# Moving h by squares in runs of 1 KB, for block 0 too, with block 0's first products reordered

## The chip, the cores and the metric

The kernel runs on one core of a Trainium2 chip. The metric is the device time of one execution in microseconds (us); before the change it is 526.12 us, the median of 3 runs (525.29 to 526.21).

The engines have short names in the profile: PE is TensorE (PEld its weight loads), DVE is VectorE, ACT is ScalarE, POOL is GpSimd, SP is SyncE, whose queue (SPq) issues most of the transfers (DMAs). Each engine works through its own instructions in order; semaphores hold an instruction until what it needs is done.

## The reference

Two layers with residuals and a layer norm after each. The input is 8192 tokens of 256 features.

```python
def _L0_attn_ref(x, W_q, W_k, W_v, W_g, W_o, log_decay):
    ...
    S = jnp.einsum('bncd,bnkd->bnck', Qc, Kc) * mask        # chunks of 32 tokens
    O = jnp.einsum('bnck,bnkd->bncd', S, Vc).reshape(B, T, D)
    gate = jax.nn.sigmoid(x @ W_g.T)
    out = gate * O @ W_o.T + x
    return out

def _L0_ffn_ref(x, w_gate, w_up, w_down):      # 768 hidden, integer weights * 1/127
    ...
    h = jax.nn.silu(gate) * up
    return jnp.einsum('bsh,dh->bsd', h, wd)

x = L0_attn_x
x = _layernorm(x + _L0_attn_ref(x, ...), axis=-1)
x = _layernorm(x + _L0_ffn_ref(x, ...), axis=-1)
```

All of it is float32. What the kernel calls h is x after the first layer norm, the input of the second layer.

## The kernel before

The tokens are worked on in 16 blocks of 512 (`TB`). A tile has the 128 partitions of the memory in front; a block of token-major data is four groups (`NG`) of 128 tokens by 256 features.

For each block the attention part makes v, y (the queries times one product of W_q and W_k), the gate, the scores (`attn_scores`, tile ps), their values (`attn_values`, po, goT) and the projection back (`attn_residual`, pa, or `split_out`, p_o). Most of these 256 x 256 products use a scheme with seven products instead of eight on halves (`seven`): first p1, p6, p5, p7, and in a second half, `rest`, three more onto the same banks. It needs sums of the input's quarters beforehand, which POOL makes (`token_sums`: t1, t3, t2, t4 on lines 444 to 447). Product p6 reads t2, the third of them.

The second layer splits its input h and its weights into a high part (32-bit) and a low part (16-bit). `ffn_up` makes, for each of six chunks of 128 hidden features, a gate bank and an up bank (fg, fu), each from two high and two low products, one for each half of the features (`dc`); the sigmoid (s, ACT), two multiplications (s and u, DVE), the high part of u (u_hi, ACT) and the low part (u_lo, POOL) follow. `ffn_down` (fdn) projects back and adds h.

`ffn_up` needs h with features on the partitions (hT), while the layer norm leaves it with tokens there. Two ways are in the kernel:

- `transpose_h`, for blocks 0 and 15: PE transposes (tile pt, eight of 128 x 128), ACT copies the high part, DVE makes the low part.
- `move_h` and `split_h`, for blocks 1 to 14: ACT normalizes h group by group (`normalize`, line 410), DVE transposes squares of 32 x 32 in place (`nc.vector.transpose`, tile sq), SP issues 16 transfers of 32 KB that bring the squares to their partitions (hT), then ACT casts the high part (line 772) and POOL makes the low part (line 773). sq and hT have one buffer each.

In `move_h` before, each transfer has for each of its 32 partitions two runs of 512 bytes on both sides.

Blocks are interleaved: while block b goes through the second layer, block b+2 has its scores, values and projection, and block b+3 its v, y and gate. Ahead of the loop, the first blocks are started by hand, and block 0's h goes by `attn_out` (its layer norm on DVE, the root on ACT) and `transpose_h`. There the order on the engines is a planner's, except where a line says `in_turn` (or `order`, which is then `in_turn`): such instructions keep the program's order. `steady` does the same for most of DVE's instructions from block 1 on. The planner also places the work of POOL and SP, so that the built order can differ from the program's.

ACT's functions come in tables that are loaded when another function is called (ACT_TABLE_LOAD); a tiny activation on the tile `table` loads one ahead of its use. `scale_and_shift` makes the factors of a layer norm from a root by ACT; `iterated_scale_and_shift` makes them on POOL with a power and one step of iteration.

PSUM has 8 banks, all from one pool (`bank`).

Of the kernel before, what the change touches and what calls it, by code (L numbers as in the profile page):

```python
# [47 lines left out]
F32 = mybir.dt.float32  # L48
# [3 lines left out]
AF = mybir.ActivationFunctionType  # L52
ALU = mybir.AluOpType

P = 128
CHUNK = 32
PAIR = 2 * CHUNK
SQ = 32
# [13 lines left out]
def kernel(  # L72
# [36 lines left out]
    def bank(name):  # L109
        return psum.tile([P, TB], F32, tag="ps", name=name)  # L110
# [190 lines left out]
    def in_turn(ins):  # L301
        tc.keep_in_program_order(ins)
# [75 lines left out]
    def iterated_scale_and_shift(mv, kind, name):  # L378
        on_r, on_dst = kind

        def column(tag):
            return small.tile([P, NG], F32, tag=tag, bufs=2, name=f"{tag}_{name}")

        def times(out, a, b):
            nc.gpsimd.tensor_tensor(out, a, b, ALU.mult)

        def line(out, a, slope, at_0):
            nc.gpsimd.tensor_scalar(out, a, slope, at_0, ALU.mult, ALU.add)

        v, y, t, minus, shift = map(  # L390
            column, ("v", "y", "t", "minus_mean", "term")
        )
        in_turn(
            nc.vector.tensor_scalar(
                v, mv[:, :, 1], 1 / on_dst**2, EPS * (on_r / on_dst) ** 2, ALU.mult, ALU.add
            )
        )
        nc.gpsimd.tensor_tensor(y, v, half, ALU.pow)
        nc.gpsimd.tensor_scalar(minus, mv[:, :, 0], -1.0, None, ALU.mult)
        times(t, y, y)  # L400
        times(t, t, v)
        line(t, t, -0.5, 1.5)
        times(y, y, t)
        times(shift, y, minus)
        return y, shift
# [33 lines left out]
    def token_sums(t, name, order=free):  # L439

        out = sums.tile([P, 4, HB], F32, tag=f"{name[0]}_sums", name=f"{name}_sums")
        t1, t3, t2, t4 = (out[:, i, :] for i in range(4))
        b11, b12, b21, b22 = (t[:, k, n * HB : (n + 1) * HB] for k in range(2) for n in range(2))
        order(nc.gpsimd.tensor_tensor(t1, b12, b11, ALU.subtract))
        nc.gpsimd.tensor_tensor(t3, b22, b12, ALU.subtract)
        nc.gpsimd.tensor_tensor(t2, b22, t1, ALU.subtract)
        nc.gpsimd.tensor_tensor(t4, t2, b21, ALU.subtract)
        return b11, b21, b22, t4, t1, t2, t3
# [173 lines left out]
    def attn_scores(b, yT):  # L622
        xt = xTs.pop(b)
        halves = [slice(i * PAIR, (i + 1) * PAIR) for i in range(P // PAIR)]
        ps = bank(f"ps_{b}")[:, : NG * PAIR].rearrange("p (g c) -> p g c", c=PAIR)
        for g in range(NG):
            for fc in range(KD):
                for rows in halves:
                    tokens = slice(g * P + rows.start, g * P + rows.stop)
                    nc.tensor.matmul(  # L630
                        ps[rows, g, :],
                        lhsT=xt[:, fc, tokens],
                        rhs=yT[:, fc, tokens],
                        start=(fc == 0),
                        stop=(fc == KD - 1),
                    )
        sTs.append(sTs.pop(0))
        sT = sTs[-1]
        for rows in halves:
            in_steady_turn(  # L640
                nc.vector.tensor_tensor(sT[rows, :, rows], ps[rows], mask[rows], ALU.mult)
            )
        return sT.rearrange("p g c -> p (g c)")
# [59 lines left out]
    def attn_out(b, goT):  # L703
        r = attn_residual(b, goT)
        layer_norm(r, f"a{b}", on_r=HALF, on_dst=H_UP)
        return r
# [33 lines left out]
    def move_h(b, h):  # L740

        sq = moved.tile([P, D // SQ, NG, SQ], F32, tag="sq", name=f"sq_{b}")
        for g in range(NG):
            in_turn(
                nc.vector.transpose(
                    sq[:, :, g, :], h[:, g, :].rearrange("p (j f) -> p j f", f=SQ)
                )  # L750
            )
        hT = moved.tile([P, KD, NQ, NG * SQ], F32, tag="hT", name=f"hT_{b}")
        for q in range(NQ):
            for j in range(NQ):
                nc.sync.dma_start(
                    hT[j * SQ : (j + 1) * SQ, :, q, :],
                    sq[q * SQ : (q + 1) * SQ, j::NQ, :, :].rearrange(
                        "p k g t -> p k (g t)"
                    ),
                )  # L760
        return hT

    def split_h(b, hT):
        hi = work.tile([P, KD, TB], F32R, tag="hT_hi", name=f"hT_hi_{b}")
        lo = work.tile([P, KD, TB], F16, tag="hT_lo", name=f"hT_lo_{b}")
        for dc in range(KD):
            whole = hT[:, dc, :, :].rearrange("p q (g t) -> p g q t", g=NG)
            in_order = [
                part[:, dc, :].rearrange("p (g q t) -> p g q t", g=NG, q=NQ)
                for part in (hi, lo)  # L770
            ]
            tc.keep_in_program_order(nc.scalar.copy(in_order[0], whole))  # L772
            nc.gpsimd.tensor_tensor(  # L773
                in_order[1], whole, in_order[0].bitcast(F32), ALU.subtract
            )
        return hi, lo


    def ffn_up(b, hT, uT, chunks, cols=slice(0, TB), held=False, order=free):

        n = cols.stop - cols.start
        for hc in chunks:
            pg = bank(f"fg_{b}_{hc}_{cols.start}")[:, :n]
            pu = bank(f"fu_{b}_{hc}_{cols.start}")[:, :n]

            kinds = (0, 1) if hc % 2 == 0 else (1, 0)
            for kind in kinds:
                for pb, w in ((pg, fg), (pu, fu)):
                    for dc in range(KD):
                        nc.tensor.matmul(  # L790
                            pb,
                            lhsT=w[kind][:, dc, hc * P : (hc + 1) * P],
                            rhs=hT[kind][:, dc, cols],
                            start=(kind == kinds[0] and dc == 0),
                            stop=(kind == kinds[1] and dc == KD - 1),
                        )
            s = work.tile([P, n], F32, tag="s", name=f"s_{b}_{hc}")
            order(nc.scalar.activation(s, pg, AF.Sigmoid, scale=SCALE / H_UP))  # L798

            gated = nc.vector.scalar_tensor_tensor(  # L800
                s, pg, U_UP / H_UP**2, s, ALU.mult, ALU.mult
            )
            in_steady_turn(gated)
            if len(uT[0]) == hc:
                for kind, dtype, tiles in zip(("hi", "lo"), (F32R, F16), uT):
                    tiles.append(
                        acts.tile([P, TB], dtype, tag=f"u_{kind}", name=f"u_{kind}_{b}_{hc}")
                    )

            def multiply(hc=hc, pu=pu, s=s):  # L810
                u = work.tile([P, n], F32, tag="u", name=f"u_{b}_{hc}")
                in_steady_turn(nc.vector.tensor_tensor(u, pu, s, ALU.mult))  # L812
                hi, lo = uT[0][hc][:, cols], uT[1][hc][:, cols]
                nc.scalar.copy(hi, u)  # L814
                nc.gpsimd.tensor_tensor(lo, u, hi.bitcast(F32), ALU.subtract)  # L815

            if held:
                return multiply
            multiply()
# [103 lines left out]
    goT = attn_values(0, sT, v, sg)  # L923
    rest()
    fd = integers(ffn_dT, ffn_int[2], "fd")
    hs[0] = attn_out(0, goT)
    sT_1 = attn_scores(1, yT)
    xTs[3] = load_xT(3)
    x_sums = token_sums(xTs[2], "x_2")
    v, rest = split_v(2, x_sums)  # L930
    goT = attn_values(1, sT_1, v_1, sg_1)
    go_sums = token_sums(goT, "go_1")
    rest()
    yT, rest = split_y(2, x_sums)
    hTs[0] = transpose_h(0, hs[0])
    in_turn(nc.scalar.activation(table, eps, AF.Sigmoid))
    rest()
    hs[1], out_rest = split_out(1, go_sums)
    sg, g_rest = split_gate(2, x_sums)
    scales_h = iterated_scale_and_shift(out_rest(), of_h, "h_1")  # L940
    ahead = yT, v, sg

# [9 lines left out]
    for b in range(NB - 2):  # L952
# [1 line left out]
        m = b + 3  # L954
        more = m < NB
        xns[n] = load_xn(n)
        hT = hTs.pop(b)
        uT = [], []
        yT, v, sg = ahead
        steady = b > 0  # L960
        if b:
            normalize(hs[b + 1], *scales_h)
            moving = move_h(b + 1, hs[b + 1])
        ffn_up(b, hT, uT, range(0, 1))
        if b == 0:
            g_rest()
            x_sums = token_sums(xTs[m], f"x_{m}")
        ffn_up(b, hT, uT, range(1, 2))
        sT = attn_scores(n, yT)
        if m + 1 < NB:  # L970
            xTs[m + 1] = load_xT(m + 1)
        ffn_up(b, hT, uT, range(2, 3))
        if b == 0:

# [283 lines left out]
```

## Time and profile before

| what | value |
|---|---|
| median of 3 runs | 526.12 us (525.29 to 526.21) |
| the profiled execution, its time | 525.69 us |
| its span, first to last instruction | 524.1 us |
| mean granted TensorE clock | 0.997 of full |
| transfers hT<-sq | 224 (16 in each of 14 blocks), 32 KB each |
| x and xT loads | 512 KB each |

How to read the profile: a row of a timeline has the start in us, the length in us, the engine, the line of the kernel, the operation, out<-in with the names of the tiles, and a count where like instructions are merged; in brackets is the idle time before it and what ended that. The row of slices has one digit for each fortieth of the span, the busy share in tenths; PEclk is the granted clock in tenths. An answer for one tile or line gives the durations in ns, as least, median and most. The chain in order of time has start, length and what held the end up in that stretch. Ends of matmuls are modelled, and they overlap in the pipeline: the pitch of two products is less than the length of one.

### The profile page before, as it was taken

How to read it: one execution, taken by the hardware profiler on the slowest of the kernel's cores; microseconds unless marked ns; L12 is line 12 of the kernel's file. 1: busy time of each engine (PE TensorE's matmuls, PEld its weight loads, DVE VectorE, ACT ScalarE, POOL GpSimd, SP SyncE). 2: the span in 40 equal slices, each digit the busy share in tenths (PEclk: the TensorE clock that was granted, in tenths of full speed). 3: DMA queues.
4: the chain of work that ended last, by engine and by line, in shares of the span. 5: the costliest groups of instructions: out<-in, count | busy, mean ns of one | idle time of the engine just before them, and what ended most of it. 6: DMA issues, size and time to landing. Idle time of an engine off the chain costs nothing.

```text
span 524.1 us, 10570 instructions
## 1 busy us (share of the span) xinstructions
PE 517.6 (99%) x3648; PEld 422.9 (81%) x3648; DVE 390.0 (74%) x963; ACT 322.4 (62%) x644; POOL 342.5 (65%) x476
## 2 busy tenths in 40 slices
PE   9999999999999999999999999999999999999995
PEld 5798887887978788887888878889787888878684
DVE  3878797676776867868677776867868677787876
ACT  2755565465656756666575665756567566667745
POOL 7435785776847668485675857668486685836554
PEclk9999999999999999999999999999999999999998
DMA  7621121212313131131312313131121311102102
GB/s 259 215 88 43 51 60 28 65 41 61 103 31 91 52 111 41 40 89 50 105 43 45 119 25 97 46 114 43 35 89 51 110 43 39 44 20 62 62 26 78
DMA packets 43320, 36.90 MB, mean 70 GB/s; under 512 B 4864, under 2 KB 39168, under 8 KB 43264
## 3 DMA queue, kind: packets, MB, share of 16 engines
q1 hardware_dynamic: 42288, 35.41, 23.1%
q10 hardware_dynamic: 976, 0.79, 0.5%
q8 instruction: 30, 0.49, 0.4%
q14 instruction: 26, 0.21, 0.1%
HBM read 20.45 MB, written 8.39 MB: 55 GB/s over the span
## 4 chain that ended last, share of the span: by engine, by line
PE 96%; DVE 2%; ACT 1%; POOL 1%; issue 0%; DVEq 0%; ACTq 0%
PE fg L790 16%; PE fu L790 16%; PE fdn L677 14%; PE p_v L473 9%; PE p_y L455 9%; PE p_g L455 9%; PE p_o L473 8%; PE po L651 5%; PE ps L630 3%; PE fdn L856 2%; PE pa L677 1%; PE pi L185 1%; PE pg L570 1%; PE pv L610 1%; PE py L589 1%; DVE st_f L322 0%
## 5 line engine op out<-in xcount | busy, mean ns | idle before, releaser
L815 POOL TENSOR_TENSOR u_lo<-u,u_hi 128x512 f16<-128x512 f32 (+1 forms) x98 | 122.9, 1256 | 111.7 <-ACT u_hi L814 109.5
L814 ACT CAST u_hi<-u 128x512 fp32r<-128x512 f32 (+1 forms) x98 | 59.7, 609 | 65.5 <-DVE u L812 65.2
L800 DVE SCALAR_TENSOR_TENSOR s<-fg,s 128x512 f32<-128x512 f32 (+1 forms) x98 | 65.9, 673 | 34.3 <-ACT s L798 34.1
L798 ACT ACTIVATE s<-fg 128x512 f32<-128x512 f32 (+1 forms) x98 | 57.0, 582 | 41.6 <-PE fg L790 41.5
L812 DVE TENSOR_TENSOR u<-fu,s 128x512 f32<-128x512 f32 (+1 forms) x98 | 66.5, 679 | 11.1 <-POOL u_lo L815 1.0
L790 PE MATMUL fg<-hT_hi,fg_hi 128*128 128x512 f32 (+1 forms) x196 | 74.0, 458 | 0.0
L790 PE MATMUL fu<-hT_hi,fu_hi 128*128 128x512 f32 (+1 forms) x196 | 60.5, 390 | 0.0
L790 PE MATMUL fg<-hT_lo,fg_lo 128*128 128x512 f16 (+1 forms) x196 | 58.0, 377 | 0.0
L790 PE MATMUL fu<-hT_lo,fu_lo 128*128 128x512 f16 (+1 forms) x196 | 57.5, 375 | 0.0
L677 PE MATMUL fdn<-fd_hi,u_hi 128*128 128x256 f32 x312 | 46.9, 292 | 0.0
L790 PEld LDWEIGHTS fu<-hT_hi,fu_hi 128*128 128x128 f32 x196 | 36.5, 188 | 8.5
L790 PEld LDWEIGHTS fg<-hT_hi,fg_hi 128*128 128x128 f32 x196 | 34.6, 189 | 8.8
L410 ACT ACTIVATE h<-h,shift_h,scale_h 128x256 f32<-128x256 f32 x52 | 27.0, 589 | 23.6 <-POOL shift_h L373 23.6
L677 PEld LDWEIGHTS fdn<-fd_hi,u_hi 128*128 128x128 f32 x312 | 39.8, 189 | 0.3
L677 PE MATMUL fdn<-fd_lo,u_lo 128*128 128x256 f16 x312 | 38.6, 273 | 0.0
L790 PEld LDWEIGHTS <-fu_lo 128*128 128x128 f16 x196 | 19.2, 98 | 22.2
L838 DVE SCALAR_TENSOR_TENSOR r<-fdn,h 128x512 f32<-128x512 f32 x30 | 20.7, 689 | 21.3 <-PE fdn L677 19.1
L773 POOL TENSOR_TENSOR hT_lo<-hT,hT_hi 128x512 f16<-128x512 f32 x28 | 35.3, 1283 | 1.2 <-ACT hT_hi L772 1.2
L790 PEld LDWEIGHTS <-fg_lo 128*128 128x128 f16 x196 | 15.3, 98 | 20.6 <-issue 12.9
L677 PEld LDWEIGHTS <-u_lo 128*128 128x128 f16 x312 | 28.4, 98 | 4.2
L473 PE MATMUL p_v<-v_sums,x_sums 128*128 128x128 f32 x240 | 31.7, 275 | 0.0
L651 PE MATMUL po<-sT,v 128*128 128x128 f32 x256 | 31.2, 275 | 0.0
(206 smaller groups left out, 1184.0 us busy)
## 6 DMA issues: line engine op xcount, KB each, us to landing
x<-in_x_dram SPq DMA_DIRECT2D x16, 512.0 KB, 3.5
xT<-in_xT_dram SPq DMA_DIRECT2D x15, 512.0 KB, 4.3
hT<-sq SPq DMA_DIRECT2D x224, 32.0 KB, 1.9
out_dram<-r SPq DMA_DIRECT2D x13, 512.0 KB, 4.7
out_dram<-r SPq DMA_DIRECT2D x8, 128.0 KB, 1.7
fg_int<-in_ffn_gT_dram SPq DMA_DIRECT2D x3, 256.0 KB, 7.9
fu_int<-in_ffn_uT_dram SPq DMA_DIRECT2D x3, 256.0 KB, 7.1
fd_int<-in_ffn_dT_dram SPq DMA_DIRECT2D x3, 256.0 KB, 6.0
```

Source lines behind the costliest of these rows:

```text
L410: nc.scalar.activation(r[:, g, :], r[:, g, :], AF.Identity, bias=shift[:, g : g + 1], scale=scale[:, g : g + 1],)
L455: nc.tensor.matmul(pb, lhsT=a[i - 1], rhs=b[i - 1], start=first, stop=True, skip_group_check=True,)
L473: nc.tensor.matmul(pb[:, g * P : (g + 1) * P], lhsT=b[i - 1][:, g * P : (g + 1) * P], rhs=a[i - 1], start=first and g == 0, stop=True, ski ...
L651: nc.tensor.matmul(po[:, cols], lhsT=v[:, g, dc * P : (dc + 1) * P], rhs=sT[:, cols], start=True, stop=True,)
L677: nc.tensor.matmul(pb[:, j * D : (j + 1) * D], lhsT=part[:, g * P : (g + 1) * P], rhs=w, start=(i == 0), stop=(i == len(terms) - 1),)
L773: nc.gpsimd.tensor_tensor(in_order[1], whole, in_order[0].bitcast(F32), ALU.subtract)
L790: nc.tensor.matmul(pb, lhsT=w[kind][:, dc, hc * P : (hc + 1) * P], rhs=hT[kind][:, dc, cols], start=(kind == kinds[0] and dc == 0), stop=( ...
L798: order(nc.scalar.activation(s, pg, AF.Sigmoid, scale=SCALE / H_UP))
L800: gated = nc.vector.scalar_tensor_tensor(s, pg, U_UP / H_UP**2, s, ALU.mult, ALU.mult)
L812: in_steady_turn(nc.vector.tensor_tensor(u, pu, s, ALU.mult))
L814: nc.scalar.copy(hi, u)
L815: nc.gpsimd.tensor_tensor(lo, u, hi.bitcast(F32), ALU.subtract)
```

## The change

- `move_h`: sq and hT are laid out so that each transfer has one run of 1 KB for each of its 32 partitions on both sides: the quarter of the features (j, or q on the other side) now stands ahead of the half (k). DVE's transposes write in that order, `split_h` reads in it. The number of transfers, their bytes and the 16 issues stay.
- Block 0's h goes the same way. Its layer norm is made by `root`, `scale_and_shift` and `normalize`; `move_h(0, ...)` stands ahead of `attn_values(1, ...)`, and `split_h(0, ...)` takes the place of `transpose_h(0, ...)`. ACT's table for the root is loaded ahead of `attn_residual(0, ...)`, and that for the sigmoids after the normalizing.
- In block 0 the second half of the gate of block 2 (`g_rest`), the token sums of block 3 and the scores of block 2 stand ahead of the first up products.
- `ffn_up` has a new mode for block 0's first two chunks: all high products of both chunks first, then the low ones. Four banks are open meanwhile.
- Some instructions on POOL get `in_turn`: the power and the negated mean of the iterated layer norm, and the second of the token sums.

The diff, cut to its core:

```diff
-        nc.gpsimd.tensor_tensor(y, v, half, ALU.pow)
-        nc.gpsimd.tensor_scalar(minus, mv[:, :, 0], -1.0, None, ALU.mult)
+        in_turn(nc.gpsimd.tensor_tensor(y, v, half, ALU.pow))
+        in_turn(nc.gpsimd.tensor_scalar(minus, mv[:, :, 0], -1.0, None, ALU.mult))
...
-        nc.gpsimd.tensor_tensor(t3, b22, b12, ALU.subtract)
+        order(nc.gpsimd.tensor_tensor(t3, b22, b12, ALU.subtract))
...
-        sq = moved.tile([P, D // SQ, NG, SQ], F32, tag="sq", name=f"sq_{b}")
+        sq = moved.tile([P, NQ, KD, NG, SQ], F32, tag="sq", name=f"sq_{b}")
         for g in range(NG):
             in_turn(
                 nc.vector.transpose(
-                    sq[:, :, g, :], h[:, g, :].rearrange("p (j f) -> p j f", f=SQ)
+                    sq[:, :, :, g, :].rearrange("p j k t -> p k j t"),
+                    h[:, g, :].rearrange("p (k j f) -> p k j f", j=NQ, f=SQ),
                 )
             )
-        hT = moved.tile([P, KD, NQ, NG * SQ], F32, tag="hT", name=f"hT_{b}")
+        hT = moved.tile([P, NQ, KD, NG * SQ], F32, tag="hT", name=f"hT_{b}")
         for q in range(NQ):
             for j in range(NQ):
                 nc.sync.dma_start(
-                    hT[j * SQ : (j + 1) * SQ, :, q, :],
-                    sq[q * SQ : (q + 1) * SQ, j::NQ, :, :].rearrange(
-                        "p k g t -> p k (g t)"
-                    ),
+                    hT[j * SQ : (j + 1) * SQ, q].rearrange("p k t -> p (k t)"),
+                    sq[q * SQ : (q + 1) * SQ, j].rearrange("p k g t -> p (k g t)"),
                 )
...
-            whole = hT[:, dc, :, :].rearrange("p q (g t) -> p g q t", g=NG)
+            whole = hT[:, :, dc, :].rearrange("p q (g t) -> p g q t", g=NG)
...
+        if hi_first:
+            for hc in chunks:
+                open_banks(hc)
+                up_products(banks[hc], hc, hT, cols, (0,), True, False)
         for hc in chunks:
...
+            if hi_first:
+                up_products(banks[hc], hc, hT, cols, (1,), False, True)
+            else:
+                open_banks(hc)
+
+                kinds = (0, 1) if hc % 2 == 0 else (1, 0)
+                up_products(banks[hc], hc, hT, cols, kinds, True, True)
+            pg, pu = banks.pop(hc)
...
-    hs[0] = attn_out(0, goT)
+    in_turn(nc.scalar.activation(table, eps, AF.Sqrt))
+    hs[0] = attn_residual(0, goT)
+    mv_h = moments(hs[0], "a0")
+    std_h = root(mv_h, "a0", HALF)
     sT_1 = attn_scores(1, yT)
+    scales_h = scale_and_shift(mv_h, std_h, of_h, "h_0")
     xTs[3] = load_xT(3)
     x_sums = token_sums(xTs[2], "x_2")
     v, rest = split_v(2, x_sums)
+    normalize(hs[0], *scales_h)
+    in_turn(nc.scalar.activation(table, eps, AF.Sigmoid))
+    moving = move_h(0, hs[0])
     goT = attn_values(1, sT_1, v_1, sg_1)
     go_sums = token_sums(goT, "go_1")
     rest()
     yT, rest = split_y(2, x_sums)
-    hTs[0] = transpose_h(0, hs[0])
-    in_turn(nc.scalar.activation(table, eps, AF.Sigmoid))
     rest()
     hs[1], out_rest = split_out(1, go_sums)
     sg, g_rest = split_gate(2, x_sums)
+    hTs[0] = split_h(0, moving)
     scales_h = iterated_scale_and_shift(out_rest(), of_h, "h_1")
...
-        ffn_up(b, hT, uT, range(0, 1))
-        if b == 0:
+        else:
+
             g_rest()
-            x_sums = token_sums(xTs[m], f"x_{m}")
-        ffn_up(b, hT, uT, range(1, 2))
-        sT = attn_scores(n, yT)
-        if m + 1 < NB:
+            x_sums = token_sums(xTs[m], f"x_{m}", in_turn)
+            sT = attn_scores(n, yT)
             xTs[m + 1] = load_xT(m + 1)
+        hT = hTs.pop(b)
+        ffn_up(b, hT, uT, range(0, 2), hi_first=not b)
+        if b:
+            sT = attn_scores(n, yT)
+            if m + 1 < NB:
+                xTs[m + 1] = load_xT(m + 1)
         ffn_up(b, hT, uT, range(2, 3))
```

The new function that both modes call:

```python
def up_products(banks, hc, hT, cols, kinds, start, stop):
    for kind in kinds:
        for pb, w in zip(banks, (fg, fu)):
            for dc in range(KD):
                nc.tensor.matmul(
                    pb,
                    lhsT=w[kind][:, dc, hc * P : (hc + 1) * P],
                    rhs=hT[kind][:, dc, cols],
                    start=(start and kind == kinds[0] and dc == 0),
                    stop=(stop and kind == kinds[-1] and dc == KD - 1),
                )
```

## The prediction

> **What bounds the kernel now.** I read the busy totals first, then the slices, the chain of waits in order of time, the timeline around block 0, and last the answers for single tiles.
>
> ```profile
> PE 517.6 (99%) x3648; PEld 422.9 (81%) x3648; DVE 390.0 (74%) x963; ACT 322.4 (62%) x644; POOL 342.5 (65%) x476
> ...
> PE   9999999999999999999999999999999999999995
> ...
> PEclk9999999999999999999999999999999999999998
> ```
>
> TensorE (PE) has work in every slice but the last, at its full clock. Every microsecond taken out of its queue is won, and every microsecond that it waits is lost, because no later gap absorbs a wait. The chain of waits says the same around block 0; these are its pieces (start, us, what):
>
> ```profile
> 41.17 0.87 PE pt L729 x8
> ...
> 48.19 0.47 PE fg L790 x2
> ...
> 50.00 1.29 PE p_g L455 x6
> ...
> 53.09 1.08 PE ps L630 x32
> ```
>
> The transposes of block 0's h (pt) hold PE for 0.87 us. Then come block 0's first up products, and inside them two pieces that don't need h: the gate's second half and the scores of block 2. The timeline gives the work that makes hT in the other blocks, and block 0's square root:
>
> ```profile
> 35.40 1.28 ACT L331 ACT_TABLE_LOAD   x1
> ...
> 37.03 0.18 DVE L342 RECIPROCAL rstd_a<-rstd_a 128x4 f32<-128x4 f32 x1 [0.88 <-ACT rstd_a L331]
> ...
> 47.95 0.71 PE L790 MATMUL fg<-hT_hi,fg_hi 128*128 128x512 f32 x2
> ...
> 52.08 1.04 POOL L398 TENSOR_TENSOR y_h<-v_h,half 128x4 f32<-128x4 f32 x1
> ...
> 61.81 10.35 SPq L755 DMA_DIRECT2D hT<-sq  x16
> ...
> 107.42 1.13 ACT L772 CAST hT_hi<-hT 128x512 fp32r<-128x512 f32 x2
> 108.40 2.53 POOL L773 TENSOR_TENSOR hT_lo<-hT,hT_hi 128x512 f16<-128x512 f32 x2
> 113.80 2.08 ACT L410 ACTIVATE h<-h,shift_h,scale_h 128x256 f32<-128x256 f32 x4 [1.78 <-POOL shift_h L373]
> 115.14 1.42 DVE L748 STREAM_TRANSPOSE sq<-h 128x256 f32<-128x256 f32 x4 [0.16 <-issue]
> 116.66 11.31 SPq L755 DMA_DIRECT2D hT<-sq  x16
> ```
>
> The long item is SP's queue: sixteen issues of 32 KB take 10.35 us. The answers for single tiles (issue times in ns, min/median/max) show why:
>
> ```profile
> L755 SPq DMA_DIRECT2D hT<-sq x224: 585/595/1790, 61.8 to 474.8; - x112
> DMA to landing us min/median/max: 1.8/1.9/3.9
> L131 SPq DMA_DIRECT2D x<-in_x_dram x16: 367/368/505, 5.6 to 424.2; - x16
> L1051 SPq DMA_DIRECT2D out_dram<-r x10: 332/332/372, 495.0 to 521.1; - x10
> ```
>
> An x load of 512 KB is issued in 0.37 us, a square of 32 KB in 0.60 us. The issue time doesn't follow bytes or the number of runs.
>
> **What the Trainium skill says.** "DMA: Bandwidth & Descriptors", Anatomy of one DMA, there for transfers that GpSimd issues: about 2 us of a transfer are fixed, mostly completion. The trace agrees for SP's: 1.9 us for 32 KB. The same page, Why small descriptors are slow (HBM only): "SBUF↔SBUF transfers don't suffer this penalty". So longer runs promise little; no run here compares them yet. "TensorE: Matmul & The Clock Gate", What's actually happening: after an idle window of about 3.4 us the clock halves. The trace shows no such gap and a clock of 0.997.
>
> **The change, part by part.** Durations are from the one profiled execution.
>
> *Removed from PE:* eight transposes, −0.87 us. *Moved on PE:* the built order puts the gate's second half and block 2's scores ahead of the first up product. They cost nothing in sum, and they are the cover of the new path. PE would reach that product, which now starts at 47.95, at 47.95 − 0.87 + 1.29 + 1.08 = 49.45.
>
> *The new path to hT_0.* The last moment of h_0 is ready at 35.24 (it starts at 35.08 and takes 0.16). The square root's table load now sits behind the fd_lo casts, which end at 32.46, so it is over by 33.9, under ACT's idle time. The root runs 35.40 to 35.70 and the reciprocal ends at 35.88. On POOL, 0.09 us of latency and three small operations (0.18 + 0.19 + 0.20) give shift at 36.54. Four normalizing passes take 2.08: 36.60 to 38.68. On DVE the last two transposes stand behind goT (0.69, from 38.05), then wait for the last passes, and end near 39.4. The first issue is at 39.45. At a pitch of (10.35 − 0.60)/15 = 0.65 us, the sixteenth is at 39.45 + 9.75 = 49.2 and lands at 51.1. The first cast (0.61) ends at 51.76, both at 52.28, both POOL differences (2.53) at 54.33.
>
> The issue of a square whose two sides are one run per partition is not in this trace. From below it is bounded by 332 ns, a store of one 1 KB run per partition; from above by 595 ns, if the saving is nothing. I take 595: the shortest of 224 is 585, so some fixed price of SBUF-to-SBUF squares fits better than a price of the runs.
>
> *What PE then waits for.* It reaches the first product at 49.45, hT_hi's first half is there at 51.8: **2.35**. The second product, 0.23 later, needs the second cast: **0.30**. Eight products at 0.23 reach the first one on hT_lo's second half at 54.17; it is there at 54.38: **0.20**. That is what the high-first order is for: without it the low products would stand right behind four high ones. Behind the casts on ACT stand block 2's gate sigmoids, wanted a block later, and sigmoid 0, which needs PE's products anyway; behind the first up product stands all of PE.
>
> *POOL.* The built order puts the two hT_lo differences, the seven small operations for h_1 and only then the token sums of block 3 on POOL. From 54.33: the power 1.01, a small one 0.19, five dependent ones at 0.28 = 1.40, three sums 0.70 + 0.70 + 0.73 = 2.13, together 59.06. PE reaches the product on the third sum at 54.38 + 7 × 0.22 + 1.90 (chunk 2) + 0.45 (four p_v) = 58.27: **0.85**. Behind these sums on POOL stand the u_lo differences; u of chunk 2 (two buffers) waits for the first, and with it the normalizing of h_1 and sigmoid 3 on ACT. Adding the same rows, DVE frees their banks some 0.5 us before PE asks, so I add nothing; if wrong, it is +0.5.
>
> Waits 2.35 + 0.30 + 0.20 + 0.85 = 3.70, less 0.87, is **+2.83 us**.
>
> *At nothing.* The 1 KB layout in the other 14 moves: hT of block 1 is complete at 61.81 + 9.75 + 1.9 = 73.5, and the cast runs at 75.40 behind sigmoids on ACT; a gain there is not on the path, and a loss of up to 1.9 us is covered. Transposes and casts with new strides: same elements, at most 0.05 us each. SP: the x load for block 3 (now at 47.83) falls behind the sixteen issues, near 50, and is needed a block later. ACT: the four passes and the sigmoid table load (1.28) end at 40.3, the copy of p_y ends at 40.95, and PE wants it at 41.0; without that cover up to +0.3. Four open banks: their last readers, the sums into h_1, end before 49. The second token sum (line 445), now in turn: in steady blocks it moves behind hT_lo, so POOL may wait 0.3 us for the cast; the sigmoids then come 0.3 later, and PE asks for their bank 3 us after. If that cover were gone, 12 × 0.3 = 3.6 us.
>
> The sum against the profiled execution (525.69, of it 524.1 span) is 528.5. It lay 0.43 under the median of the runs, so I add 2.83 to 526.12 instead.
>
> **The rivals.**
>
> *A, likeliest:* issues stay near 0.6 us; 528.9, between 527.9 (latencies a little shorter) and 530.3 (covers of 0.3 and 0.5 fail).
>
> *B, not slower:* an issue falls towards 332 ns, because both sides become one run. At a pitch of 0.385 the last square lands at 39.45 + 5.78 + 1.9 = 47.1; ACT is free at 47.95, the casts and differences end at 48.55 and 51.1, PE waits for neither, and only the sums are late by about 0.3. That gives −0.87 + 0.3 = −0.57: 525.5. For: stores of such runs take 332. Against: loads with many pieces take 368, so pieces explain only 36 of 263 ns. It decides from a pitch of 0.48 us down: then the waits together fall under 0.87.
>
> *C, slower still:* the squares go at block 2's pitch, (11.31 − 0.60)/15 = 0.71, 1.0 us later in all. PE's gap becomes 3.4 us, enough for the clock to halve by the skill's page; an estimate from it: one window of 3.4 us at half speed loses 1.7. Total +2.8 + 1.0 + 1.7 = 5.5: 531.6. Against: 0.65 is the pitch where no other DMA ran.
>
> *D, the change doesn't do what it says:* the layout gives no faster transfer anywhere. It is part of A and C; the time is theirs.
>
> **How the numbers follow.** A 0.70, B 0.18, C 0.10, anything else 0.02. Within 0.2% (1.05 us) is about what a measurement of this kernel can't tell from no change. B's own values lie between −0.6 and +1.0, so nearly all of B is "same"; 0.04 is left for faster, if a wait I priced isn't there and steady blocks gain. Slower: A and C, 0.80. The range goes from B's 525.4 to 530.6, which leaves out C and half of the rest. A's own range is 527.9 to 530.3.
>
> **What would show it.** Right: in the changed profile PE has a gap of 2 to 3 us before the first fg, released by ACT's hT_hi; sixteen issues still take over 9 us; a second gap of under 1 us stands before p_v, released by POOL's token sums; the rest is as before, only later. Wrong: issues near 0.35 us; a first fg without a wait; or gaps in blocks 1 to 14.

## The result, and the profile after

The changed kernel takes 531.04 us (median of 5 runs, 530.70 to 531.27), the kernel before 525.97 in the same comparison (5 runs, 525.16 to 526.21). The ratio is 1.0104, with a 95% interval of 1.0093 to 1.0116: 5.1 us slower, where +2.8 was predicted; the time lies 0.4 us above the predicted range.

The page of the profiled execution (531.04 us, span 529.4), same lines as before:

```profile
PE 518.3 (98%) x3640; PEld 422.3 (80%) x3640; DVE 390.8 (74%) x960; ACT 322.7 (61%) x649; POOL 346.1 (65%) x481
...
PE   9998999999999999999999999999999999999993
...
PEclk9999899999999999999999999999999999999997
```

PE has eight products less (the transposes). It loses time in two places only: the fourth slice, with a lower clock in the fifth, and the last one, where a 5 has become a 3. Everything between is as it was.

The chain of waits around block 0 (start, us, what):

```profile
48.61 1.83 DMA hT<-sq
50.44 0.02 issue
50.46 0.04 ACTq L772
50.50 0.04 issue
50.54 0.63 ACT hT_hi L772
51.16 0.04 issue
51.21 0.49 PE fg L784
```

The chain now runs through the sixteenth square and the first cast into the first up product, as predicted. The timeline has the same path with what each engine waited for:

```profile
34.93 0.30 ACT L331 ACTIVATE rstd_a<-mv_a,eps 128x4 f32<-128x4 f32 x1
...
36.26 2.07 ACT L410 ACTIVATE h<-h,shift_h,scale_h 128x256 f32<-128x256 f32 x4 [0.27 <-POOL shift_h L373]
...
39.10 10.10 SPq L757 DMA_DIRECT2D hT<-sq  x16
...
50.54 1.14 ACT L772 CAST hT_hi<-hT 128x512 fp32r<-128x512 f32 x2 [2.72 <-DMA hT<-sq]
...
51.21 1.02 PE L784 MATMUL fg<-hT_hi,fg_hi 128*128 128x512 f32 x2 [1.86 <-ACT hT_hi L772]
51.23 1.29 POOL L773 TENSOR_TENSOR hT_lo<-hT,hT_hi 128x512 f16<-128x512 f32 x1 [4.00 <-ACT hT_hi L772]
```

Sixteen issues still take 10.10 us; PE idles for 1.86. The answer for the squares' line (issue ns, min/median/max):

```profile
L757 SPq DMA_DIRECT2D hT<-sq x240: 507/589/1890, 39.1 to 477.3; - x120
```

The median issue fell from 595 to 589 ns: one run instead of two per partition saves 6 ns, not 263.

Up to the end of DVE's chain the change costs about what was predicted. In the trace, the way from the first product of po (block 0's values; its time varies by a microsecond between executions, so it serves as zero) to the copy of the count into n_wide takes 494.41 us before and 497.51 after: **+3.10**. The two ends of that way, before and then after:

```profile
26.55 1.95 PE L651 MATMUL po<-sT,v 128*128 128x128 f32 x16
...
520.96 0.13 DVE L1192 CAST n_wide<-count 1x1 int32<-1x1 f32 x1
```

```profile
26.20 1.95 PE L651 MATMUL po<-sT,v 128*128 128x128 f32 x16
...
523.71 0.13 DVE L1218 CAST n_wide<-count 1x1 int32<-1x1 f32 x1
```

From there to the last instruction it was 3.11 us and is now 5.71: **+2.60**. The head was 0.35 us quicker in this execution, and 3.10 + 2.60 − 0.35 = 5.35 is the whole difference of the two spans. The second part is in no step of the prediction.

What stands there: the kernel ends with a branch. Each engine reads n_wide, the count of a rare case, and jumps over a long piece of code that treats that case; here it always jumps. The two branch instructions of PE's sequencer, before and then after (ns, min/median/max of the two; start of the first and last):

```profile
L1196 PEldq COMPARE_BRANCH  x2: 95/246/397, 521.9 to 522.2; - x2
```

```profile
L1222 PEldq COMPARE_BRANCH  x2: 95/1794/3493, 524.7 to 525.0; - x2
```

The jump, the second of the two, took 0.40 us before and 3.49 after. SP's queue waits for it before the program ends. Its waits there, before and after (us in total, times, longest):

```profile
SPq L1254 <- PEq L1254: 0.7, 2, 0.5
```

```profile
SPq L1280 <- PEq L1280: 3.3, 2, 2.8
```

The DMA queues tell why. q8 carries PE's instructions, to judge by its spacing: 30 packets, 0.49 MB in all, so 16 KB each, one for about 256 of PE's 7,385 records (7,368 after). From 516 us to the end of its jump at 522.6 the kernel before fetched one, 5.7 us ahead of the jump:

```profile
q1 hardware_dynamic: 576, 0.52, 23.5%
q8 instruction: 1, 0.02, 0.9%
```

The changed kernel's jump runs from 524.97 to 528.47. From 516 to 525.5 there is no q8 packet; one comes while the jump runs (window 525.5 to 528.5). The two windows:

```profile
q1 hardware_dynamic: 863, 0.79, 24.2%
q14 instruction: 1, 0.01, 0.4%
```

```profile
q8 instruction: 1, 0.02, 2.5%
q14 instruction: 1, 0.01, 1.0%
```

The Trainium skill describes this ("Runtime: NRT & Kernel Launch", Instruction fetch mechanics): instructions come in 16 KiB blocks of 256, fetched ahead in sequence, and a taken branch whose target isn't among the blocks at hand waits for a fetch. The packets agree in size and spacing. The theory was then: PE's program is 17 records shorter (8 loads, 8 products, 1 semaphore), so PE no longer enters its last block ahead of the jump, the block behind that isn't fetched, and the target lies in it.

### The profile page after: what moved, and what is told of

It reads as the page before. It is cut to its first block, busy times and chain, and to the rows that moved or that the text cites. A ratio compares the mean times of both kernels' runs of the same rounds, so it can differ in the third digit from the quotient of the medians.

```text
span 529.4 us, 10591 instructions
## 1 busy us (share of the span) xinstructions
PE 518.3 (98%) x3640; PEld 422.3 (80%) x3640; DVE 390.8 (74%) x960; ACT 322.7 (61%) x649; POOL 346.1 (65%) x481
## 4 chain that ended last, share of the span: by engine, by line
PE 92%; DVE 3%; SPq 2%; ACT 1%; POOL 1%; issue 0%; DMA 0%; DVEq 0%; ACTq 0%
PE fg L784 16%; PE fu L784 16%; PE fdn L677 14%; PE p_v L473 8%; PE p_y L455 8%; PE p_g L455 8%; PE p_o L473 8%; PE po L651 5%; PE ps L630 3%; PE fdn L873 2%; SPq L757 2%; PE pa L677 1%; PE pi L185 1%; PE pg L570 1%; PE pv L610 1%; PE py L589 1%
## 5 line engine op out<-in xcount | busy, mean ns | idle before, releaser
L815 ACT ACTIVATE s<-fg 128x512 f32<-128x512 f32 (+1 forms) x98 | 55.8, 581 | 40.5 <-PE fg L784 39.1
L410 ACT ACTIVATE h<-h,shift_h,scale_h 128x256 f32<-128x256 f32 x56 | 29.1, 590 | 26.4 <-POOL shift_h L373 26.4
L773 POOL TENSOR_TENSOR hT_lo<-hT,hT_hi 128x512 f16<-128x512 f32 x30 | 37.8, 1281 | 8.9 <-ACT hT_hi L772 8.9
```

The lines of the kernel that those rows point to most:

```text
L410: nc.scalar.activation(r[:, g, :], r[:, g, :], AF.Identity, bias=shift[:, g : g + 1], scale=scale[:, g : g + 1],)
L773: nc.gpsimd.tensor_tensor(in_order[1], whole, in_order[0].bitcast(F32), ALU.subtract)
```

## The experiments

Times are compared with runs of the kernel before on the same chip: 525.46 for e1 to e4, 525.65 for e5 to e8, 525.56 for e9 to e11.

**e1, eight idle products at PE's end**

```diff
+    pad = bank("pad")
+    for _ in range(8):
+        in_turn(nc.tensor.matmul(pad[:1, :1], lhsT=nc.const_aps.tensor(1.0, [P, 1], BF16), ...))
     n_wide = const.tile([1, 1], I32, tag="n_wide", name="n_wide")
```

> The changed kernel with eight matmuls of one column added behind its last product, ahead of the count's branch, where PE is idle for 2.4 us. Theory F (fetch): the 2.5 us at the very end come from PE's last branch, whose target has to be fetched because PE's program is 17 instructions shorter; 16 more put it back. Then PE's branch takes 0.4 us as before instead of 3.49, and the time falls by 2.5 to about 528.5; the 2.6 us around block 0 stay. Theory S (stores or queues): the end is longer because the last stores or SP's longer program are late; then eight idle matmuls change nothing, 531.0.

Measured: 530.95 (530.82 to 531.27), ratio 1.0103 (1.0088 to 1.0118). PE's branch still took 3.28 us. Theory F's number was missed, S's was met. But the trace again has no q8 packet from 516 us to the jump, so the eight were perhaps too few; e2, e5 and e9 decide. This execution also answers another question. Its products ran at full clock behind the gap, the changed kernel's at half. The windows of one microsecond (PE, PEld, DVE, ACT, POOL busy; then PEclk), the changed kernel's and then e1's:

```profile
53.00:54.00 1.00, 1.00 (x3) 0.43 (x2) 0.00 (x0) 0.00 (x0) 1.00 (x2) 0.50 0.84 324
54.00:55.00 1.00, 1.00 (x4) 0.41 (x4) 0.00 (x0) 0.00 (x0) 1.00 (x3) 0.50 0.07 20
55.00:56.00 1.00, 1.00 (x4) 0.36 (x3) 0.21 (x1) 0.60 (x1) 0.72 (x4) 0.50 0.00 0
```

```profile
54.00:55.00 1.00, 1.00 (x6) 0.40 (x5) 0.00 (x0) 0.11 (x1) 1.00 (x2) 1.00 0.54 201
55.00:56.00 1.00, 1.00 (x7) 0.50 (x6) 0.48 (x1) 0.73 (x2) 0.92 (x4) 1.00 0.00 0
```

From po to n_wide the changed kernel takes 497.51 us and e1 497.16. So the half clock costs 0.35 us here, not 1.3; what it hides is seen in e9.

**e2, the kernel before with 36 idle products at PE's end** (the same edit, `range(36)`, nothing else)

> The kernel before with 36 matmuls of one column added behind its last product, in PE's idle time (2.4 us), and nothing else. Theory F, in its stricter form that only the block of 256 instructions ahead is there when PE branches: the branch moves 72 instructions on, its target (some 450 further) falls into a block not yet fetched, the branch takes about 3.5 us and the time rises by 2.5 to 3 us, to 528.5 to 529. Theory S: nothing at the end but up to 0.6 us if the 36 matmuls outlast the idle time; 526.0 to 526.6.

Measured: 528.53 (528.43 to 529.04), ratio 1.0057 (1.0044 to 1.0070): +3.1. The branch:

```profile
L1208 PEldq COMPARE_BRANCH  x2: 95/1870/3645, 522.5 to 522.8; - x2
```

Nothing that the kernel computes was touched, and no data moves differently. From po to n_wide it takes 494.40 us, as before; behind n_wide it takes 5.86 instead of 3.11. Here a q8 packet did come ahead of the jump, at 516.9, and a second one, at 523.7, while it ran, which fits a target beyond the block fetched ahead. The place of PE's jump in its program is worth 3 us. Theory S falls.

**e3, the layout alone** (the diff's lines in `move_h` and `split_h` on the kernel before)

> The kernel before with the new layout of the squares alone (blocks 1 to 14; block 0 stays on the transposes). My theory: an issue stays at 0.585 to 0.60 us and nothing on PE's path changes: 526.0 within 0.5. Rival (layout pays or costs): transfers with 1 KB runs finish earlier and something in the steady blocks gains, 14 x 0.1 us or more, 524.5 or less; or the transposes with the new stride are slower and cost as much.

Measured: 525.40 (13 runs), ratio 0.9998 (0.9990 to 1.0006). The q1 packets fell from 42,288 to 35,120, and the time stayed. The squares' line:

```profile
L756 SPq DMA_DIRECT2D hT<-sq x224: 507/589/1570, 61.7 to 474.6; - x112
```

**e4, PE's gap filled**

```diff
         hT = hTs.pop(b)
+        if b == 0:
+            fill = bank("fill")
+            for _ in range(9):
+                in_turn(nc.tensor.matmul(fill, lhsT=nc.const_aps.tensor(1.0, [P, P], BF16), ...))
         ffn_up(b, hT, uT, range(0, 2), hi_first=not b)
```

> The changed kernel with nine bf16 matmuls of 512 columns on constants (about 2.0 us) put on PE between the scores of block 2 and the first up product, where PE waits for 1.9 us. They keep PE busy in the gap, so no window at half clock should follow; their 18 instructions also put the end back under theory F (-2.5). Theory H (the half clock is a loss of its own): block 0 gets 1.3 us faster, the offset against before falls from 2.6 to about 1.3, time about 527.2. Theory P (POOL's chain behind hT_lo sets the time, the half clock only hides it): the products run faster but PE then waits at block 3's token sums, the waits I predicted (0.20 and 0.85); the offset stays at 2.4 to 2.8, time about 528.4.

Measured: 530.29, but in two groups: 528.07 and 528.61, and four runs from 530.15 to 531.23. The two are near theory P's value, but were not profiled. The profiled execution is of the other group, and not for its end (a branch of 0.41 us): its last square, issued at 49.47, wasn't there until 53.4, so that the fill was followed by the same gap. ACT's cast and PE's first product in its timeline:

```profile
53.49 1.14 ACT L772 CAST hT_hi<-hT 128x512 fp32r<-128x512 f32 x2 [4.83 <-DMA x<-in_x_dram]
```

```profile
54.16 1.31 PE L784 MATMUL fg<-hT_hi,fg_hi 128*128 128x512 f32 x2 [1.91 <-ACT hT_hi L772]
```

One q8 packet was under way just then (4.8% of 16 engines in 50.7 to 52.5, so 1.4 us of one engine), and the x load for block 3 had been issued at 50.17. Which of them held the square up was not tried. As a test of H against P, e4 alone is inconclusive.

**e5, nine instead of eight**

> As e1, but nine idle matmuls of one column instead of eight. Theory F: PE's records before the branch then number 7386; kernels with 7385 and 7387 fetched the last block before they branched, those with 7368 and 7384 did not, so the limit lies between 7384 and 7385 and one more matmul takes the branch from 3.3 to 0.4 us: about 528.2, that is 2.7 above the kernel before on the same chip. Theory S, or a cause that only goes with the change: as e1, 5.5 above it.

Measured: one run at 528.61, five from 531.20 to 531.99; the profiled one has a branch of 3.63 us. The sharp limit that I had read from the counts doesn't exist: the same program falls on either side. The reading that fits is that its end lies right at a block's limit, and that an execution fetches the last block ahead of the jump or doesn't; the quick run was not profiled. e6, e7 and e8 have nine idle products too, and their profiles have a quick jump (0.415 us each) behind a q8 packet.

**e6, five of the sixteen squares issued by ACT**

```diff
-                nc.sync.dma_start(...)
+                if later is not None and NQ * q + j >= 11:
+                    later.append(pair)     # issued by nc.scalar, in turn, between ACT's copies
+                else:
+                    nc.sync.dma_start(*pair)
```

> As e5, and the last five of block 0's sixteen squares are issued on ACT's queue between its copies, so that SP issues eleven. Nothing else is moved. My theory (the serial issue at 0.63 us on one queue is what makes PE wait): the last square lands near 48, PE reaches the first up product without a wait, what is left is the late token sums of block 3 (0.3 to 0.9 us); about 525.8, or 0 to 0.7 above the kernel before. Rival (landing or ACT's casts set it, or the DMAs on ACT delay its copies): the gap stays over 1 us, 527 or more.

Measured: two groups again, 11 runs from 525.15 to 526.62, around the expected 525.8, and 11 from 528.52 to 529.62. e10 takes the second group away, and is shown instead.

**e7, block 0 without the high-first order** (`hi_first` left out)

> As e5, but the first two chunks of block 0 in the order of the kernel before (chunk 0 high then low, chunk 1 low then high); same number of instructions. My theory: PE reaches the first low product four products earlier, 0.9 us after the first high one, while hT_lo's two halves come 1.3 and 2.5 us after the casts: it waits about 1.0 us more there, and half of that is given back since the token sums are then waited for less. 0.3 to 1.0 us slower than e5. Rival: the token sums set the time in both, no difference.

Measured: five runs from 529.70 to 530.53 and one at 533.64. The profiled one, of the five, has a short branch (0.415 us). The five are compared with e9, which has the high-first order and a short branch, each by its distance from the kernel before on its chip: 4.5 and 3.0, so 1.5 slower, more than I expected. PE's timeline:

```profile
54.70 0.58 PE L784 MATMUL fg<-hT_lo,fg_lo 128*128 128x512 f16 x1 [0.84 <-POOL hT_lo L773]
```

The wait for hT_lo's second half is there with 0.84 (expected 1.0). A window at half clock followed in this execution (54.64 to 58.05), so the rest of the 1.5 isn't told apart.

**e8, the token sums of block 3 ahead of hT_lo on POOL** (`g_rest()` and `token_sums` called ahead of `split_h`)

> As e5, but block 3's token sums stand on POOL ahead of hT_lo and of the seven small operations for h_1 (POOL is idle there for 4 us); the gate's second half moves ahead of the last p_o products on PE, in sum nothing. Theory P (in block 0 PE waits for the squares and then for the token sums, and a window of half clock only hides the second): the sums' wait is gone and the time falls by 0.6 to 0.9 against e5 where the clock stays full; where it is halved for 3.4 us the loss of 1.3 comes back, so runs spread over 0 to 0.9 faster. Theory H (the half clock alone makes the rest of block 0's loss): no run faster than e5 by more than 0.2.

Measured: 527.61 and 527.97, and four runs from 530.02 to 530.88. The profiled one (527.97) has a short branch, full clock and no wait of PE for the sums. The four were not profiled; they lie about 1 us below e5's slow group. By the distance from the kernel before, the pair is 0.8 quicker than e9, as theory P says; H expected no gain.

**e9, twenty idle products at PE's end**

> As e1 and e5, but with twenty idle matmuls of one column. Theory F, mended after e5 (with 7384 to 7386 records PE's program ends right at the limit of a block, and whether the last block is fetched before the branch differs from run to run): 40 instructions put the branch clearly behind the limit, and its target, 23 instructions further than in the kernel before, still lies in the fetched block (e2 lost it at 72 further). Every run then has a branch of 0.4 us: 528.2 to 528.8, 2.6 to 3.0 above the kernel before, with a spread under 1 us. If the branch is still slow in some runs, the limit is no matter of PE's instruction count.

Measured: 528.55, all five runs from 528.40 to 528.78; ratio 1.0060 (1.0046 to 1.0074), +3.0. The branch is as before the change:

```profile
L1234 PEldq COMPARE_BRANCH  x2: 95/246/397, 524.8 to 525.1; - x2
```

Twenty products that compute nothing make the changed kernel 2.5 us quicker (e1, with eight, lay 5.5 above the kernel before). It isn't the idle products as such: in e9 they shorten the jump, in e2 they lengthen it. Together the two show that the end is set by where the jump stands in PE's program.

All thirteen profiles fit a jump that waits for a fetch. In the four with a slow jump (the changed kernel, e1, e2, e5) a q8 packet starts about 1 us after the jump does, and the jump ends 1.4 us after the packet. In the other nine one starts 4.2 to 6.1 us ahead of the jump, and none while it runs. From n_wide to the last instruction the nine take 3.10 or 3.11 us, the four 5.49 to 5.86.

PE's only waits in block 0:

```profile
51.72 1.02 PE L784 MATMUL fg<-hT_hi,fg_hi 128*128 128x512 f32 x2 [1.86 <-ACT hT_hi L772]
58.88 1.38 PE L473 MATMUL p_v<-v_sums,x_sums 128*128 128x128 f32 x10 [0.64 <-POOL x_sums L446]
```

This is the predicted pair: the first up product on the cast, p_v on the token sums. Where the clock halves, PE comes to p_v later and the second wait isn't seen.

**e10, e6 with twenty idle products**

> As e6 (five of block 0's squares issued on ACT's queue), with twenty idle matmuls instead of nine. Theory F: the slower half of e6's runs (528.5 to 529.6) is gone, all runs lie with its faster half, 525.2 to 526.1: the kernel before within 0.4. PE has no gap before block 0's first up product; its only wait there is 0.4 us for the token sums of block 3. If theory F fails, two groups of runs remain.

Measured: 525.90 (21 runs, 525.20 to 526.76), ratio 1.0006 (0.9999 to 1.0012). One group. PE goes from the scores into the up products with no gap, and waits once:

```profile
48.33 1.15 PE L630 MATMUL ps<-yT,xT 128*64 128x64 f32 x32
49.41 0.73 PE L788 MATMUL fg<-hT_hi,fg_hi 128*128 128x512 f32 x2
...
55.95 1.60 PE L473 MATMUL p_v<-v_sums,x_sums 128*128 128x128 f32 x12 [0.41 <-POOL x_sums L446]
```

The 2.6 us of e9 over e10 are what the serial issue on one queue cost.

**e11, e10 with the token sums ahead of h_1's small operations**

> As e10, and on POOL the order hT_lo, token sums of block 3, then the seven small operations for h_1. The last wait of 0.4 us goes, and PE has eight transposes less than the kernel before (0.87): 0.3 to 0.9 below the kernel before, 524.7 to 525.3. Rival: the normalizing of h_1, now 2.9 us later, is waited for in block 1, and nothing is won.

Measured: 525.91 (13 runs), ratio 1.0008 (1.0000 to 1.0017). A miss: nothing won. The wait for the sums is gone, and another has come 13 us later:

```profile
69.42 0.70 PE L455 MATMUL p_y<-x_sums,m_sums 128*128 128x256 f32 x2 [0.34 <-DVE p_y L508]
```

Of the 0.88 us that the transposes freed, 0.34 go there and 0.45 into small starts between products (0.18 from p_o to the first up product, the rest between it and fdn). Behind that the remaining 0.09 is lost too: from po to n_wide e11 takes 494.61 us, the kernel before 494.41; where, was not followed up. No version tried is quicker than the kernel before.

## Why the prediction was right in block 0 and wrong at the end

Point by point, with the changed kernel's profile, and e9's where the clock stayed full:

| step | predicted | measured |
|---|---|---|
| PE's transposes gone | −0.87 | −0.88 (po to p_o: 16.63, now 15.75) |
| first issue | 39.45 | 39.10, with the head 0.35 earlier: exact |
| pitch of the issues | 0.65 | (48.61 − 39.10)/15 = 0.63 |
| last square landed | 51.1 | 50.44 |
| wait for the first cast | 2.35 | 51.21 − (48.20 + 1.08) = 1.93 |
| second product on the second cast | 0.30 | 0.52 − 0.22 = 0.30 |
| hT_lo's second half | 0.20 | 0.12 (e9: 0.56 for two products instead of 0.44) |
| token sums at p_v | 0.85 | 0.64 (e9) |
| blocks 1 to 14, layout | 0 | 0 (e3) |
| the end behind n_wide | 0, unpriced | +2.60 |

**Right:** the likeliest case A, the price of an issue, and what becomes of it. e9 is the changed kernel without the change at the end, and it stands at +3.0 (predicted +2.83). That is partly luck: the four waits came to 2.99 instead of 3.70, and 0.6 us in no term of mine filled most of the difference (from po to n_wide e9 takes 497.11 us, 2.70 more than before, where 2.99 − 0.88 is 2.11). About half of the 0.6 are small starts between products up to block 0's fdn; the rest was not found. Rival B fell with the issue at 589 ns. Rival D was right as to the layout.

**Rival C** ends near the measured time (531.6) by another mechanism. The pitch was 0.63 and the gap 1.9 us, not 0.71 and 3.4. The clock did halve, for 3.41 us, in the changed kernel's profiled execution; in e1's, with the same gap, it didn't. The page of the skill that the prediction drew on ("TensorE: Matmul & The Clock Gate", What's actually happening) also says that the activity window runs free, and the traces agree: in each, the clock changes only at whole multiples of 3.413 us after its first rise (the changed kernel's at 4.97, then 14 and 15 such windows later). In the seven profiles with a gap ahead of the first up product, what decides is how PE's idle time falls into these windows. In the changed kernel 1.86 us of idle PE fell into one window, in e4 1.91, in e7 1.67 (two gaps), and the next window ran at half. In e1, e5, e8 and e9 the limit of a window cut the same gap in two, with at most 1.37 us in one, and the clock stayed full. I had taken 3.4 us as the gap's own threshold, and had read the clock of 0.997 as no halving at all; in the kernel before it halves too, at 521.15, when PE has run out of work. The halving cost little here: the way from po to n_wide is 497.51 us with it and 497.16 in e1.

**The step that failed** is the sentence "the rest is as before, only later", and ahead of it the sum that was closed at the last product. The chain of waits of the kernel before ended with n_wide, and the span at 524.1:

```profile
521.05 0.05 DVE n_wide L1192
```

Three microseconds behind the last computation were in plain view, and I did not ask what filled them. Removing eight transposes was priced as −0.87 on PE; that it also moves PE's jump, and what the jump needs, was no term. The term measures 3.49 − 0.40 = 3.1 on PE, of which 2.6 show at the end, as SP was busy with its own waits for the first 0.5 (in the kernel before they end at 523.2, when PE's jump had been over since 522.6).

**Open:** why the same program (e5 to e8) has the block fetched ahead of the jump in some executions and, by their times, not in others. The count of PE's records alone doesn't decide it: the kernel before has 7,385, between e1's 7,384 and e5's 7,386, and none of its 79 runs beside the experiments was slow (526.42 at most). Open, too, is what held the last square up in e4.

## What to carry to other kernels

Before a change is priced, close the profile's sum at the last instruction, not at the last product: a program that ends with a jump can have a term that depends on how many instructions stand ahead of it, here on PE, so that removing or adding some can cost or win 3 us that have nothing to do with what the edit computes. To test it, pad the engine's idle end with empty instructions and read the time of the branch; do that first, so that other experiments don't carry the jump along. The path of sixteen small transfers cost queue time for each issue, in both layouts: count issues by pitch, and if such a path is late, split it over two queues before rearranging bytes.

## What was not expected of the hardware

- A jump whose target wasn't fetched took 3.28 to 3.65 us on PE (four profiles), one whose target was there 0.40 to 0.42 (nine). The target lies some 450 instructions ahead by a count of the program (no trace shows it), and with the jump moved 72 instructions on (e2) it was lost, which fits two blocks of 256 at hand.
- Idle products of one column take about 0.03 us each (36 of them 1.04 us in e2, within PE's idle time), and are a means to place a jump.
- The clock changes on a grid of 3.413 us. Where 1.67 us or more of PE's idle time fell into one window of that grid, the next window ran at half clock (three profiles); where it was 1.37 us or less, it didn't (four). The halving cost 0.35 us of the whole.
- The issue of a 32 KB square between partitions takes 0.59 us with one run per partition and 0.595 with two; ACT's queue issues it in about the same time (0.52 to 0.60 for single ones in e6).
